# Second FFN of a macaron block: normalized rows stored by quarters and turned on VectorE instead of TensorE

## The chip, the cores and the metric

The kernel runs on one core of a Trainium2 chip. A core has TensorE for matmuls (PE in the profile; PEld is its loading of weights, which overlaps the matmuls), VectorE (DVE), ScalarE (ACT), GpSimd (POOL), and SyncE (SP), which here only issues DMAs. Each engine works through its own queue of instructions in order and waits on semaphores for the others. Matmuls write to PSUM, which here is cut into eight banks of 128 x 512 floats; everything else lives in SBUF (128 partitions) or in DRAM. The metric is the time of one execution in microseconds.

## The reference

2048 rows of 1024 channels go through three residual steps. `ffn` and `attn` normalize their input by row first.

```
x = x + 0.5 * ffn(layernorm(x))
x = x + attn(layernorm(x))
x = x + 0.5 * ffn(layernorm(x))

ffn(x):   routing = softmax(x @ gate_w.T)                 # 8 experts
          out = (x * (routing @ in_channel_scale)) @ sign(weight).T
          out = out * (routing @ out_channel_scale) + bias
attn(x):  3-tap convolution 1024 -> 768, split in q, k, v of 256
          16 heads of 64, causal softmax attention inside blocks of 128 rows
          o @ wo, then @ proj_w + proj_b                  # back to 1024 channels
```

The two FFNs use the same weights. Everything is float32; the large FFN product takes its rows in two float32r parts, a high one and a low one.

## The kernel before

The rows are handled in 16 tiles t of 128 rows (`NT` = 16), the channels in 8 chunks of 128 (`DC` = 8). The first FFN runs over the tiles, its normalized output goes through the convolution (a fast algorithm with eight products), and then come the attention and the second FFN, which the change touches.

**Attention.** It has four groups g of four tiles, and per group four turns r, each of which handles four heads (two head pairs). `turn(g, r, ...)` issues the stages of several pairs at once, staggered: `stage_qk` (q and k by seven products, accumulated in two banks "mm" and two banks "tr" and evicted by ScalarE, `put`, and VectorE, `more`), `stage_wo` of an earlier pair, `stage_transpose`, `stage_scores` (scores, masking on GpSimd, maxima on VectorE, exps on ScalarE, normalization on VectorE), `stage_values`. In turn 1 of group g, `stage_proj` finishes the previous group: for each of its four tiles two products `pp` with `proj_w`, which VectorE adds to the row tile `xr` in SBUF (L1116); the sum goes to DRAM as `x3[t]` (L1119). The row tiles are loaded by `load_residual` into the pool `rring` (4 buffers), and the DMAs of GpSimd add `proj_b`. In the same turn `signs` loads two chunks of the FFN weights into the pool `aside` (2 buffers), and ScalarE takes their signs.

**Second FFN.** `Ffn` (L188) does for each tile:

- `norm`: load the row tile from `x3` (`load_rows2`, L928), statistics on VectorE (L167, L171, L173), the power -0.5 and the shift on GpSimd (L174, L185), the normalized row `xn` on ScalarE (L186);
- `add_bias`: a DMA of GpSimd adds `hbias` to the row tile in place (L212);
- `transpose`: 8 TensorE transposes of 128 x 128 into two PSUM banks (L220), copied by ScalarE to `xnT` (L221), a tile with channels on partitions, in a pool of three buffers;
- `gate`, `route`, `turn`: the router's logits (`lgp` L228, `lg` L241), their maximum `nm` and softmax (VectorE and ScalarE), its weights `rhl` in two parts (L252, L253), turned by one TensorE transpose `rt` (L260) and copied to `rT` by VectorE (L262);
- `scale`: the input scales `is` by matmul (L272); VectorE multiplies `xnT` by them in place (L283), ScalarE rounds the product to the high part of `y` (L285), GpSimd subtracts to get the low part (L286); the output scales `po` (L295) are halved by ScalarE (L297);
- `main`: 32 matmuls `pm` of 128 x 512 (L311) in two halves of the output columns; VectorE multiplies by the output scale (L323) and adds to the row (L324); `store` writes the tile out.

`run` puts these stages in a software pipeline. In the turn of tile t:

```python
self.on(self.gate, t + 2)             # if not done yet
self.scale(t + 1, out=True)
self.main(t, 0)
self.on(self.route, t + 2)
self.on(self.transpose, t + 3)
self.on(self.norm, t + 4, t < self.kept)
self.on(self.add_bias, t + 4)
self.main(t, 1, beside={DC - 2: lambda: self.on(self.turn, t + 2)})
```

The first tiles' stages are written by hand between the stages of the last attention pairs (`ffn.transpose(0, ...)`, `ffn.gate(0)` and so on). Row tiles of the second FFN live in nine buffers: 2 of `aside`, 3 of a pool `rring2`, 4 of `rring`.

**What sets the order.** TensorE's order is written by hand (`manual_schedule`). The other engines' queues are filled by a planner that takes instructions by program order, priority and its own estimate of when each is ready; so an instruction may move ahead of others on its engine. A tile in a pool gets the buffer of the tile that many places before it, and its first writer waits for the last reader of that one.

## Time and profile before

| | |
|---|---|
| median of three runs | 940.13 us (940.07 to 940.71) |
| the profiled execution | 940.06 us, span 938.3 us |
| granted TensorE clock | 1.00 of full speed |
| 0 to 200 us, first FFN: TensorE busy | 189.6 us |
| 200 to 540 us, convolution and the start of attention: TensorE busy | 337.9 us |
| 540 to 740 us, attention: TensorE busy, of each 40 us | 39.7 to 40.0 us |
| second FFN in its steady part, one tile (pm at 900.61 to pm at 910.49) | 9.88 us |
| transposes of the second FFN on TensorE | 128, of 273 ns each, overlapping |

The span is what the profiler recorded from the first to the last instruction of one execution; about 1.8 us of the time lie around it. A line of the timeline gives the start and the duration in us, the engine, the line of the kernel, the operation, output<-input, shapes and a count, and in brackets how long the engine had idled and for whom. Consecutive instructions of one kind are merged, with the time from the first's start to the last's end. A line of groups gives a count, the busy time in us and the mean in ns of one. Matmul rows are pipelined, so their durations overlap: what one costs is read from the starts around it. L numbers are those of this kernel.

### The profile page before, as it was taken

Reading aid. Unit: us, or ns where it says so; the run is one execution under the profiler, and the core shown is the slowest. Engines: PE = TensorE matmul, PEld = TensorE weight load, DVE = VectorE, ACT = ScalarE, POOL = GpSimd, SP = SyncE. Lnnn points to the kernel's source line nnn. Section 1 sums busy time; section 2 is a strip of 40 time slices with the busy share of each in tenths; the row PEclk is TensorE's granted clock in tenths of the full one; section 3 lists DMA queues with packets and bytes.
Section 4 is the critical chain, followed back from the end, with each engine's and each line's share of the span. In section 5 each row is a group of like instructions: output and inputs, shape, how many; then the busy total and the mean of one; then the engine's idle time right before and its main releaser. Section 6 shows DMA issues by size and latency. Waiting matters only on the chain.

```text
span 938.3 us, 14525 instructions
## 1 busy us (share of the span) xinstructions
PE 920.0 (98%) x5240; PEld 659.5 (70%) x5240; DVE 662.3 (71%) x1326; ACT 462.0 (49%) x1258; POOL 235.7 (25%) x330
## 2 busy tenths in 40 slices
PE   6999999999999999999999999999999999999998
PEld 4678878886666666675876577567765756788786
DVE  5888887789978677656686557656746666666654
ACT  5676666431111111126886567666855844454441
POOL 2554453220011100101231113013201404444341
PEclk9999999999999999999999999999999999999999
DMA  9776653499567765536360245032406737655341
GB/s 343 181 199 192 178 182 136 186 274 353 181 201 195 190 188 135 117 108 222 116 135 23 75 154 133 23 140 89 88 1 209 150 114 210 172 163 152 90 114 67
DMA packets 39543, 144.86 MB, mean 154 GB/s; under 512 B 5096, under 2 KB 6120, under 8 KB 37552
## 3 DMA queue, kind: packets, MB, share of 16 engines
q1 hardware_dynamic: 28048, 97.91, 28.9%
q0 software_dynamic: 10688, 38.02, 20.9%
q10 hardware_dynamic: 736, 8.02, 2.3%
q8 instruction: 41, 0.67, 0.3%
q14 instruction: 30, 0.25, 0.1%
HBM read 89.30 MB, written 37.85 MB: 136 GB/s over the span
## 4 chain that ended last, share of the span: by engine, by line
PE 80%; DVE 7%; ACT 6%; DMA 3%; issue 3%; POOL 1%; POOLq 0%; DVEq 0%; ACTq 0%
PE cv L544 23%; PE pm_f L311 19%; PE pq L829 7%; PE pp L1108 6%; PE pv L829 5%; PE acc L1084 4%; PE sc L1012 3%; PE tr_f L220 3%; PE pt L1054 2%; DMA x<-in_x_dram 2%; ACT p L1039 2%; PE ao L1067 2%; PE lgp_f L228 2%; PE is_f L272 1%; ACT qk L972 1%
## 5 line engine op out<-in xcount | busy, mean ns | idle before, releaser
L311 PE MATMUL pm_f<-sw,y_f 128*128 128x512 f32 x1024 | 258.4, 403 | 0.6 <-ACT y_f L285 0.4
L311 PEld LDWEIGHTS pm_f<-sw,y_f 128*128 128x128 f32 x1024 | 186.8, 190 | 41.9 <-ACT y_f L285 0.8
L544 PE MATMUL cv<-v,u 128*128 128x342 f32 x576 | 166.0, 450 | 0.0
L544 PEld LDWEIGHTS cv<-v,u 128*128 128x128 f32 x576 | 109.2, 190 | 56.7
L1025 POOL TENSOR_SCALAR_AFFINE_SELECT p<-p 128x512 f32<-128x512 f32 x64 | 38.5, 635 | 249.6 <-ACT p L1021 249.6
L1039 ACT ACTIVATE p<-p,anm 128x128 f32<-128x128 f32 x256 | 99.8, 396 | 0.0
L561 ACT ACTIVATE m<-cv 128x342 f32<-128x342 f32 x42 | 19.2, 456 | 154.4 <-PE cv L544 152.3
L323 DVE TENSOR_TENSOR pm_f<-pm_f,os_f 128x512 f32<-128x512 f32 x64 | 44.6, 697 | 68.6 <-PE pm_f L311 68.5
L286 POOL TENSOR_TENSOR y_f<-xnT_f,y_f 128x512 fp32r<-128x512 f32 x63 | 80.0, 1288 | 45.3 <-ACT y_f L285 45.3
L1035 DVE TENSOR_REDUCE anm<-p 128x4 f32<-128x512 f32 x64 | 39.6, 678 | 26.9 <-POOL p L1025 26.9
L1084 PE MATMUL acc<-oT,wo_sb 128*128 128x512 f32 x128 | 58.0, 595 | 0.2 <-DVE oT L1076 0.2
L544 PE MATMUL cv<-v,g 128*128 128x342 f32 (+2 forms) x224 | 57.1, 415 | 0.8 <-DVE v L466 0.8
L1108 PE MATMUL pp<-pw_sb,o2T 128*128 128x512 f32 x128 | 56.4, 596 | 0.0
L221 ACT COPY xnT_f<-tr_f 128x512 f32<-128x512 f32 x58 | 33.6, 588 | 41.6 <-PE tr_f L220 39.9
L544 PEld LDWEIGHTS cv<-v,g 128*128 128x128 f32 x224 | 39.7, 190 | 17.6 <-DVE v L466 1.2
L1039 ACT ACTIVATION_READ_ACCUMULATOR p<-p,anm 128x1 f32 x256 | 49.9, 195 | 0.0
L1059 DVE COPY pT<-pt 128x512 f32<-128x512 f32 x32 | 22.1, 690 | 38.8 <-PE pt L1054 38.8
L972 ACT ACTIVATE qk<-pq,sbq 128x256 f32<-128x256 f32 x64 | 30.0, 469 | 39.5 <-PE pq L829 39.5
L1047 DVE TENSOR_TENSOR p<-p,asum 128x512 f32<-128x512 f32 x64 | 45.1, 704 | 1.3
L1108 PEld LDWEIGHTS pp<-pw_sb,o2T 128*128 128x128 f32 x128 | 23.7, 190 | 29.1 <-issue 26.1
L297 ACT ACTIVATE os_f<-po_f 128x512 f32<-128x512 f32 x64 | 34.8, 595 | 16.8 <-PE is_f L272 6.7
L285 ACT CAST y_f<-xnT_f 128x512 fp32r<-128x512 f32 x64 | 37.6, 626 | 11.1 <-DVE xnT_f L283 11.1
(186 smaller groups left out, 1668.0 us busy)
## 6 DMA issues: line engine op xcount, KB each, us to landing
g<-in_conv_w_dram SPq DMA_DIRECT2D x28, 512.0 KB, 5.2
u<-in_conv_w_dram POOLq DMA_DIRECT2D x24, 512.0 KB, 6.1
x<-in_x_dram SPq DMA_DIRECT2D x16, 512.0 KB, 5.5
raw<-in_weight_t_dram SPq DMA_DIRECT2D x16, 512.0 KB, 6.5
x<-hbias POOLq DMA_DIRECT2D x16, 512.0 KB, 5.3
x<-x SPq DMA_DIRECT2D x16, 512.0 KB, 4.1
xr<-x SPq DMA_DIRECT2D x16, 512.0 KB, 4.9
xr<-in_proj_b_dram POOLq DMA_DIRECT2D x16, 512.0 KB, 9.1
```

Source lines behind the costliest of these rows:

```text
L286: lows[h].tensor_tensor(yl, y, yh.bitcast(F32), ALU.subtract)
L311: ins = nc.tensor.matmul(pms[h], lhsT=y[:, n, c, :], rhs=self.sw[:, c, ts(h, NB)], start=(c == 0 and n == 0), stop=(c == DC - 1 and n == 1),)
L323: nc.vector.tensor_tensor(pms[h], pms[h], o, ALU.mult)
L544: nc.tensor.matmul(accs[w, k][:, lo:hi], lhsT=uk[:, c, :], rhs=V[k][:, c, lo:hi], start=(c == 0), stop=(c == DC - 1),)
L829: nc.tensor.matmul(leave.sums[sums], lhsT=rows[a][:, u, :], rhs=cols[b], start=n in (0, 1, 3), stop=True, skip_group_check=True,)
L972: nc.scalar.activation(h, acc, AF.Identity, bias=bias, scale=(QSCALE, 1.0)[n])
L1025: nc.gpsimd.affine_select(out=p, in_=p, pattern=[[0, BPG], [-1, P]], compare_op=ALU.is_ge, fill=NEG_INF, base=0, channel_multiplier=1,)
L1035: nc.vector.tensor_reduce(nmax, p, AX.X, ALU.max, negate=True)
L1039: exps[g, r] = nc.scalar.activation(p[:, b, :], p[:, b, :], AF.Exp, bias=nmax[:, b : b + 1], accum_out=asum[:, b : b + 1],)
L1047: nc.vector.tensor_tensor(p, p, asum.unsqueeze(2).broadcast_to([P, BPG, P]), ALU.mult)
L1084: nc.tensor.matmul(accs[g][m], lhsT=wo_sb[:, hp, ts(m, P)], rhs=oT, start=(hp == 0), stop=(hp == NHP - 1),)
L1108: nc.tensor.matmul(pp, lhsT=o2T[:, m, ts(b, P)], rhs=pw_sb[:, m, ts(h, NB)], start=(m == 0), stop=(m == WC - 1),)
```

## The change

The rows are no longer normalized in the second FFN but in attention, right after `stage_proj` has finished them: VectorE takes the statistics of `xr` there (`row_statistics`), and ScalarE writes the normalized row to a tile `xp`, in an order that puts quarters of 32 channels of each chunk together. Four DMAs per tile store `xp` to DRAM (`quarters[t]`) so that quarter q of all channels lies on partitions 32q to 32q + 31. The second FFN loads such a tile (`xl`, three buffers) in one DMA, and two VectorE instructions per tile turn it in blocks of 32 x 32, which gives the same `xnT` as the eight TensorE transposes and two copies did. The row tiles `xf` have seven buffers instead of nine, since `xp` and `xl` take room; `aside` holds `xp` in the first three groups, and two buffers of a new pool in the last one. In the compiled kernel VectorE's two transposes of a tile often stand well ahead of their place in the program, as the planner sets them.

```diff
--- before.py
+++ after.py
@@ -368,6 +368,42 @@
 
 
 
+    class Second(Ffn):
+        def load(self, t):
+            xl = self.xns[t] = self.xnp.tile([P, 4, DC, QC], F32, name=f"xl_{self.name}_{t}", tag="xn")
+            nc.sync.dma_start(out=xl, in_=quarters[t].rearrange("p (t j a) -> p t j a", t=4, j=DC))
+        def transpose(self, t):
+            xl = self.xns.pop(t)
+            xnT = self.work.tile([P, DC, P], F32, name=f"xnT_{self.name}_{t}", tag="xnT", bufs=3)
+            blocks = xnT.rearrange("p j (t b) -> p t j b", t=4)
+            for k in range(2):
+                nc.vector.transpose(blocks[:, ts(k, 2)], xl[:, ts(k, 2)])
+            self.xnTs[t] = xnT
+        def run(self, first):
+            for t in range(first, self.end):
+                self.on(self.gate, t + 2)
+                if t + 1 < self.end:
+                    self.scale(t + 1, out=True)
+                self.main(t, 0)
+                self.on(self.route, t + 2)
+                self.on(self.transpose, t + 3)
+                self.on(self.beside, t + NT - 2)
+                self.on(self.ahead, t + 4)
+                self.main(t, 1, beside={DC - 2: lambda: self.on(self.turn, t + 2)})
+                self.on(self.after, t - 1)
     NK = 8
     SCALES = (1.0, -2.0 / 9, -2.0 / 9, 1.0 / 90, 1.0 / 90, 1.0 / 180, 1.0 / 180, 1.0)
     PAIRS = ((1, 2), (3, 4), (5, 6))
@@ -922,13 +958,13 @@
     f2 = ctx.enter_context(ExitStack())
     rring = pool(b3, "rring", BPG)
     aside = pool(b3, "aside", 2)
-    rows, x3 = {}, {}
+    rows, x3, quarters = {}, {}, {}
     later = []
 
     def load_rows2(t):
         if t in rows:
             return
-        pl = aside if t % 9 < 2 else later[0] if t % 9 < 5 else rring
+        pl = aside if t % 7 < 2 else later[0] if t % 7 < 3 else rring
         rows[t] = pl.tile([P, D], F32, name=f"xf_{t}", tag="x")
         nc.sync.dma_start(out=rows[t], in_=x3[t])
 
@@ -1100,6 +1136,45 @@
                 pin(nc.sync.dma_start(out=rows[t], in_=x2[t]))
                 pin(nc.gpsimd.dma_start(out=rows[t], in_=proj_b.broadcast_to([P, D]), accum_op=ALU.add))
 
+        finish = {}
+        def row_statistics(t):
+            src = rows[t]
+            stats = small.tile([P, NH2, 6], F32, name=f"st_f2_{t}", tag="stats")
+            for h in range(NH2):
+                nc.vector.bn_stats(out=stats[:, h, :], in_=src[:, ts(h, NB)])
+            mv = small.tile([P, 2], F32, name=f"mv_f2_{t}", tag="mv")
+            nc.vector.bn_aggr(out=mv, in_=stats)
+            rstd = small.tile([P, 1], F32, name=f"rs_f2_{t}", tag="rstd")
+            nc.vector.tensor_scalar(rstd, mv[:, 1:2], EPS, None, ALU.add)
+            nc.gpsimd.tensor_tensor(rstd, rstd, nhalf, ALU.pow)
+            shift = small.tile([P, 1], F32, name=f"sh_f2_{t}", tag="shift")
+            nc.gpsimd.tensor_scalar(shift, mv[:, 0:1], rstd, -1.0, ALU.mult, ALU.mult)
+            def normalized():
+                pl = later[1] if t + BPG >= NT else aside
+                xp = pl.tile([P, D], F32, name=f"xp_{t}", tag="x")
+                nc.scalar.activation(
+                    xp.rearrange("p (q j a) -> p j q a", q=4, j=DC),
+                    src.rearrange("p (j q a) -> p j q a", q=4, j=DC),
+                    AF.Identity,
+                    bias=shift,
+                    scale=rstd,
+                )
+                quarters[t] = spill.tile([P, D], F32, name=f"xq_{t}")
+                to = quarters[t].rearrange("(q b) c -> b q c", q=4)
+                for k in range(4):
+                    nc.sync.dma_start(
+                        out=to[:, :, ts(k, D // 4)],
+                        in_=xp[ts(k, QC), :].rearrange("b (q c) -> b q c", q=4),
+                    )
+            finish[t] = normalized
         def stage_proj(g, b, kinds=("mm", "tr")):
             o2T = accs[g]
             for h in range(NH2):
@@ -1115,6 +1190,7 @@
                 xt = rows[g * BPG + b][:, ts(h, NB)]
                 stored[g] = nc.vector.tensor_tensor(xt, pp, xt, ALU.add)
             t = g * BPG + b
+            row_statistics(t)
             x3[t] = spill.tile([P, D], F32, name=f"x3_{t}")
             nc.sync.dma_start(out=x3[t], in_=rows.pop(t))
 
@@ -1139,6 +1215,9 @@
             if r == 1 and g + 1 < NG:
                 tokens_of(g + 1)
             stage_qk(g, r)
+            if r > 1 and g > 0:
+                with tc.high_priority(offset=300):
+                    finish.pop((g - 1) * BPG + r)()
             if r == 0 and g > 0:
                 load_residual(g - 1)
             if r == 1:
@@ -1162,52 +1241,51 @@
             if r == 1 and g > 0:
                 for b in range(BPG):
                     stage_proj(g - 1, b)
+                    if b > 1:
+                        finish.pop((g - 1) * BPG + b - 2)()
 
         with tc.manual_schedule(engines={mybir.EngineType.PE}):
             for i in range(LAST - 1):
                 turn(*divmod(i, NP), True)
-                if i == LAST - 3:
-                    for t in range(2):
-                        load_rows2(t)
                 if i == LAST - 2:
                     load_residual(NG - 1)
             g, r = pairs[-1]
-            begun = {}
-            xn_of = {}
+            stage_qk(g, r)
+            with tc.high_priority(offset=300):
+                finish.pop(g * BPG - 1)()
             for t in range(2):
-                with tc.issue_after(stored[g - 1].ins):
-                    begun[t] = sums_of(
-                        lambda t=t: xn_of[t], rows[t], f"f2_{t}", on_vector=t, later=True
-                    )
-            stage_qk(g, r)
+                load_rows2(t)
 
             b2.close()
             pool(f2, "edge2", 1, side="right").tile([P, 120], F32, name="right_edge2")
             work = pool(f2, "work2", 2, side="right")
-            xn2 = pool(f2, "xn2", 3, side="right")
-            later.append(pool(f2, "rring2", 3, side="right"))
-            ffn = Ffn("f2", sw2, work, xn2, 0, NT, lambda t: rows[t], load_rows2, store, lambda t: None, lambda t: None, NT, leave)
+            xlp = pool(f2, "xl2", 3, side="right")
+            later.append(pool(f2, "rring2", 1, side="right"))
+            later.append(pool(f2, "xp2", 2, side="right"))
+            def begin_tile(t):
+                ffn.load(t)
+                load_rows2(t)
+                ffn.add_bias(t)
+            def finish_row(t):
+                finish.pop(t, lambda: None)()
+            ffn = Second("f2", sw2, work, xlp, 0, NT, lambda t: rows[t], begin_tile, store, None, finish_row, NT, leave)
+            for t in range(3):
+                ffn.load(t)
             two(stage_wo, LAST - 3)
             two(stage_transpose, LAST - 2, "sm", "tr")
-            for t in range(2):
-                ffn.xns[t] = xn_of[t] = xn2.tile([P, D], F32, name=f"xn_f2_{t}", tag="xn")
-                begun[t]()
-
-            def begin_tile(t):
-                ffn.norm(t, t > 0)
-                ffn.add_bias(t)
-
-            on_vector = (nc.vector.tensor_copy,) * 2
+            ffn.transpose(0)
             stage_scores(g, r)
             with tc.high_priority(offset=400):
                 two(stage_values, LAST - 2)
             for t in range(2):
                 ffn.add_bias(t)
-            ffn.transpose(0, on_vector)
             two(stage_wo, LAST - 2)
             ffn.gate(0)
             stage_transpose(g, NHP - 2, "sm")
-            ffn.transpose(1, on_vector)
+            ffn.transpose(1)
             stage_values(g, NHP - 2)
             stage_transpose(g, NHP - 1, "mm")
             stage_wo(g, NHP - 2)
@@ -1216,16 +1294,19 @@
             ffn.gate(1, "tr")
             stage_wo(g, NHP - 1)
             with tc.issue_after(ended[g].ins):
-                begin_tile(2)
+                load_rows2(2)
+                ffn.add_bias(2)
             one = ("mm", "mm")
             stage_proj(g, 0, one)
             ffn.turn(0)
             ffn.transpose(2)
             stage_proj(g, 1, one)
             ffn.scale(0, out=True)
+            finish_row(NT - 4)
             ffn.route(1)
             stage_proj(g, 2, one)
             stage_proj(g, 3, one)
+            finish_row(NT - 3)
             ffn.turn(1)
             begin_tile(3)
     ffn.run(0)
```

## The prediction

> **What bounds the kernel now.** I read the page's busy times first, then the timeline of the second FFN, then that of the attention stage in front of it, and last the waits.

> ```profile
> PE 920.0 (98%) x5240; PEld 659.5 (70%) x5240; DVE 662.3 (71%) x1326; ACT 462.0 (49%) x1258; POOL 235.7 (25%) x330
> PEclk9999999999999999999999999999999999999999
> PE 80%; DVE 7%; ACT 6%; DMA 3%; issue 3%; POOL 1%; POOLq 0%; DVEq 0%; ACTq 0%
> ```

> TensorE is busy for 98% of the span at full granted clock: work taken from it shortens the run, unless a wait takes its place. So the question is what TensorE's order will wait for. The timeline of the second FFN shows two tiles that differ in just what the change touches. At 904.52 stand the last eight transposes; the tile that starts at 910.49 (t = 13) has none, and no normalization beside it:

> ```profile
> 904.38 0.28 PE L241 MATMUL lg_f<-fold,lgs_f 128*128 128x8 f32 x2
> 904.52 1.07 PE L220 MATMUL tr_f<-ident,xn_f 128*128 128x128 f32 x8
> 905.34 3.01 PE L311 MATMUL pm_f<-sw,y_f 128*128 128x512 f32 x12
> ...
> 910.49 3.93 PE L311 MATMUL pm_f<-sw,y_f 128*128 128x512 f32 x16
> 910.77 1.28 DVE L283 TENSOR_TENSOR xnT_f<-xnT_f,is_f 128x512 f32<-128x512 f32 x2
> 912.33 2.53 POOL L286 TENSOR_TENSOR y_f<-xnT_f,y_f 128x512 fp32r<-128x512 f32 x2 [7.16 <-ACT y_f L285]
> 914.26 0.28 PE L241 MATMUL lg_f<-fold,lgs_f 128*128 128x8 f32 x2
> 914.40 2.99 PE L311 MATMUL pm_f<-sw,y_f 128*128 128x512 f32 x12
> 914.46 0.70 DVE L323 TENSOR_TENSOR pm_f<-pm_f,os_f 128x512 f32<-128x512 f32 x1 [2.41 <-PE pm_f L311]
> ...
> 916.28 0.29 DVE L253 SCALAR_TENSOR_TENSOR rhl_f<-ro_f,rsum_f,rhl_f 128x64 fp32r<-128x64 f32 x1
> 917.23 0.27 PE L260 MATMUL rt_f<-ident,rhl_f 128*128 128x128 f32 x1
> ```

> From the lg matmul to the next pm matmul it is 0.96 us with transposes and 0.14 without: eight cost 0.82 us. The routing weights rhl are ready at 916.57 and TensorE takes them (rt) at 917.23: 0.66 us in hand, no more. GpSimd ends its subtractions, the last readers of xnT, at 914.86.

> **The change, part by part.** The sum is made against the profiled run's 940.06 us (span 938.3 and 1.8 around it), the median of the runs shown being 940.13.

> *Transposes off TensorE.* 16 tiles x 0.82 = -13.1 us, 3 of the tiles before the loop, 13 in it. ScalarE also loses 1.24 + 2 x 0.59 us a tile in this stage, where it idles anyway: nothing.

> *Transposes on VectorE, in the loop.* Two 128x512 instructions a tile. No row shows one. Bounds: 0.54 us (TENSOR_SCALAR 128x512, SBUF to SBUF, mean 542) and 1.22 (SCALAR_TENSOR_TENSOR 128x1024, mean 1216, as if each element took two cycles). I take 0.64, the pace of BATCH_NORM_STATS2, which also reads 512 elements of SBUF and takes 1.28 for two. They replace 1.28 + 0.21 + 0.15 us of statistics, so VectorE's load hardly changes; their place does. In the compiled order of VectorE the two transposes of tile t+4 stand directly behind the two multiplications of tile t+1 (L283), ahead of the pm multiplication, in t = 1, 3 and 5 to 11. xnT has three buffers, so tile t+4 writes where tile t+1 lies, and must wait until GpSimd's second subtraction has read it. Counted from the tile's first pm matmul: GpSimd ends at 914.86 - 910.49 = 4.37; handing over takes 0.06, the transposes 1.28, to 5.71; from the start of the pm multiplication to the end of rhl it took 2.11 (914.46 to 916.57), to 7.82, and 0.05 to TensorE: 7.87. TensorE is at rt at 917.23 - 910.49 = 6.74. It waits 1.13 us, which is 0.31 more than the transposes cost. The four pm matmuls behind rt, and with them the next tile, move along. Nine tiles: +10.2. In t = 4 the planner puts 14 instead of 12 pm matmuls ahead of rt, which leaves 0.65. In t = 0 is_1 comes after four pm matmuls, so GpSimd ends later: 1.8. In t = 2 the pair stands around the pm multiplication of half 1, costs no rt wait, but delays by 0.64 the multiplications that t = 3 then waits for: +0.64. Together +13.3 (5.7 us more or less for each 0.25 us of one transpose).

> [...]

> *Start of the FFN.* VectorE does six transposes ahead of oT_6 where it did four copies (mean 669): +1.2 us; and the maxima anm_3_1 now stand behind the reciprocal of p_6_0's sums, which holds the exps back by 1.0. By the rows from 747.72 on I get the ao_7 matmuls 2.0 us later than before, though 1.64 us of TensorE transposes are gone ahead of them: 3.6 lost. Then the first transpose of tile 3 stands ahead of the second pp_2 addition and waits for GpSimd's subtractions of tile 0 (2.49 long); pp_3's second matmuls need that PSUM bank: 2.2. With the statistics of rows 14 and 15 between, rT_1 comes 0.8 later. Together +6.6. Bounds: 0 (other work covers it all) and 10, if the first quarters loaded land 3 us late: 3.5 MB of loads at 98 MB per 271 us (28.9% of the span) take 10 us and share the engines with the proj_b additions.

> *Attention, groups 1 to 3.* VectorE gets 1.28 + 0.21 + 0.15 us of statistics a row beside the pp additions, ScalarE one normalization a row (1.24), SP four stores of 128 KB a row and later a load (0.32 us each to issue).

> ```profile
> 620.78 0.68 DVE L1047 TENSOR_TENSOR p<-p,asum 128x512 f32<-128x512 f32 x1
> ...
> 628.14 0.69 DVE L1116 TENSOR_TENSOR xr<-pp,xr 128x512 f32<-128x512 f32 x1 [1.02 <-PE pp L1108]
> 629.86 0.69 DVE L1116 TENSOR_TENSOR xr<-pp,xr 128x512 f32<-128x512 f32 x1 [1.02 <-PE pp L1108]
> ...
> 630.29 0.47 ACT L972 ACTIVATE qk<-pq,sbq 128x256 f32<-128x256 f32 x1 [6.92 <-PE pq L829]
> 630.96 0.59 PE L829 MATMUL pq<-x,wk_sb 128*128 128x256 f32 x2
> ```

> VectorE is busy without a gap until 623.7 and then has 1.02 us free per addition of 1.72; the 1.64 a row fits two such gaps, but row 0's share adds to the busy stretch. Followed through, the last pp addition ends at 631.8 instead of 630.55, and the pq matmul at 630.96 needs its bank: 0.9 us a group, 2.7 in all. ScalarE's first two normalizations fall into its 6.92 us of idling; the third stands among the qk evictions, where it idles 1.69; the fourth delays a copy of scores by 1.24, but the probabilities it holds back are multiplied behind the column sums (655.65) in two groups and have 0.4 us and TensorE's earlier pt to spare in the third: nothing. If this cover fails, each costs 1.24 us, 14.9 for twelve. Bounds 0 and 14.9; I take 2.7, since the backlog follows from rows of this stage. GpSimd's 0.56 + 0.26 a row and the selects queued behind them: it idles 26.64 us there. What waits on SP behind the stores are residual loads and tokens needed ten microseconds and more later; the third normalization needs its `aside` buffer back from the stores, 2.6 us to land by the output's row.

> *Row buffers.* Nine become seven: xf of t+7 waits for the store of t (2.6), its load (4.5), then GpSimd's bias DMA (0.90), which stands ahead of y. From 0.4 into the next tile that leaves some 3 us before GpSimd is needed. Costed at nothing; later than that, it costs one for one on about six tiles. The quarters are loaded more than a tile ahead, 4.5 us in tiles of 10.

> Sum: 940.1 - 13.1 + 13.3 + 6.6 + 2.7 = 949.6. I say 949.5.

> **The rivals.** *The waits stay off the path (faster).* If the transposes let the pm multiplication through, because GpSimd ends earlier or the instruction is very short, the 13.1 us stay: with the attention's 2.7 and a quarter of the start (1.6), 931.3. For it: VectorE has 2.41 us free ahead of the pm multiplication. Against it: GpSimd's end at 4.37 lies 0.4 behind that multiplication's start (3.97). The point that decides: waits below (13.1 - 9.3) / 11.5 = 0.33 us a tile.

> *The transpose takes 1.22 us.* VectorE's chain to rt grows by 1.16: 11.5 x 1.16 = 13.3 more in the loop and 2.3 at the start: 965. Nothing but the missing row speaks for it.

> *Attention pays more.* If half of the normalizations fall on the path, or the small stores return `aside` late, 7.5 us more, with 1 for late quarters: 958. For it: ScalarE is busy 5.00 of 5.00 us around 615 and 645. Against it: its idle times above.

> *It cancels.* With 0.54 us a transpose and the start free, 940 - 13.1 + 10 + 2.7 = 940: no change.

> **How the numbers follow.** My case 0.53 (its own range 944 to 956), waits off the path 0.22, dear transpose 0.08, dear attention 0.12, cancelled 0.05. About 0.2%, 1.9 us, is what a measurement of this kernel can tell from no change. Faster: 0.22 and 0.02 of the cancelled: 0.24; same 0.05; slower 0.71. The range 932 to 962 leaves out half of the fast rival and most of the dear transpose, some 0.18.

> **What would show it.** Right: no tr_f in the second FFN; transposes of about 0.6 to 0.7 us on VectorE that idle for GpSimd first; TensorE's rt waiting some 1.1 us for rhl in nine tiles; tiles of about 10.2 us against 9.88; pp_3 and oT_6 late. Wrong: tiles near 9.1 us with rt not waiting; a transpose far from 0.64; TensorE gaps in the attention stage over 3 us a group; a bias DMA of GpSimd, or a load of quarters, ahead of the wait.

## The result

The changed kernel takes 954.18 us (median of 4 runs, 953.63 to 955.24) against 940.1 us before (939.93 to 940.71, 4 runs): a ratio of 1.015 with a 95% interval of 1.0132 to 1.0168. It is slower, as forecast, and 4.7 us slower than the 949.5 forecast, inside the range. The profiled execution took 954.39 us, with a span of 952.6. Below, "shift" is the start of an instruction on TensorE in this trace, minus the start of the same instruction in the trace of before.

From the page of the changed kernel, the lines that answer to those shown of before: busy times, the granted TensorE clock in 40 slices, and the chain that ended last by engine.

```profile
PE 913.5 (96%) x5112; PEld 649.3 (68%) x5112; DVE 671.9 (71%) x1353; ACT 451.8 (47%) x1231; POOL 236.2 (25%) x331
PEclk9999999999999999999999999999999999989999
PE 69%; DVE 9%; DMA 7%; issue 6%; POOL 5%; ACT 5%; SPq 0%; POOLq 0%; DVEq 0%; ACTq 0%
```

TensorE has 128 instructions less, as it should, but its share of the chain falls from 80% to 69%. More of the chain now runs over VectorE (9% for 7), DMA (7 for 3), GpSimd (5 for 1) and "issue" (6 for 3). One slice of the clock line is new too: the 8.

A steady tile of the second FFN (the turn t = 9, whose rt belongs to tile 11) in the timeline of the changed kernel:

```profile
885.35 1.28 DVE L283 TENSOR_TENSOR xnT_f<-xnT_f,is_f 128x512 f32<-128x512 f32 x2
886.98 2.53 POOL L286 TENSOR_TENSOR y_f<-xnT_f,y_f 128x512 fp32r<-128x512 f32 x2 [2.93 <-ACT y_f L285]
888.83 0.28 PE L241 MATMUL lg_f<-fold,lgs_f 128*128 128x8 f32 x2
888.96 2.99 PE L311 MATMUL pm_f<-sw,y_f 128*128 128x512 f32 x12
889.54 1.31 DVE L387 STREAM_TRANSPOSE xnT_f<-xl_f 128x512 f32<-128x512 f32 x2 [2.91 <-POOL y_f L286]
890.77 0.67 DVE L323 TENSOR_TENSOR pm_f<-pm_f,os_f 128x512 f32<-128x512 f32 x1
...
892.56 0.28 DVE L253 SCALAR_TENSOR_TENSOR rhl_f<-ro_f,rsum_f,rhl_f 128x64 fp32r<-128x64 f32 x1
...
892.99 0.30 PE L260 MATMUL rt_f<-ident,rhl_f 128*128 128x128 f32 x1 [1.04 <-DVE rhl_f L253]
```

VectorE idles 2.91 us for GpSimd's subtractions, with the pm multiplication queued behind the transposes; when those are through, rhl comes 1.04 us too late for TensorE. From lg to the next pm matmul it is now 0.13 us instead of 0.96. A tile takes 10.24 us (rt at 882.75 and 892.99) against 9.88 before.

The largest single loss lies elsewhere, in t = 4. First GpSimd's part of the timeline, then TensorE's, then windows of two microseconds (length, TensorE's busy time and instructions, granted clock, DMA share, GB/s):

```profile
828.05 0.86 POOL L212 DMA_DIRECT2D xf<-hbias  x1 [3.48 <-issue]
834.10 0.86 POOL L212 DMA_DIRECT2D xf<-hbias  x1 [5.19 <-DMA xf<-x]
834.66 2.83 POOL L286 TENSOR_TENSOR y_f<-xnT_f,y_f 128x512 fp32r<-128x512 f32 x2
```

```profile
840.84 0.45 PE L260 MATMUL rt_f<-ident,rhl_f 128*128 128x128 f32 x1 [3.92 <-DVE rhl_f L253]
```

```profile
838.00:840.00 2.00, 0.00 (x0) 0.93 1.05 258
840.00:842.00 2.00, 1.16 (x3) 0.50 0.74 244
842.00:844.00 2.00, 2.00 (x27) 0.50 0.52 190
844.00:846.00 2.00, 2.00 (x7) 0.50 0.98 193
846.00:848.00 2.00, 2.00 (x9) 0.86 0.99 324
```

A bias DMA of a later tile stands ahead of the subtractions of tile 5 in GpSimd's queue. It waits until 834.10 for the load of its row, the subtractions begin at 834.66 (with the bias DMA behind them, as the run `bias_behind_y` has it, they begin at 831.90), and everything of the steady chain follows from there: TensorE stands for 3.92 us. Its clock is granted at half from 839.7 to 846.6, most of that after it has started again.

The start of the second FFN in the changed kernel, VectorE first, then TensorE, and last the same ao matmuls in the kernel before, where they waited for nothing:

```profile
757.80 0.71 DVE L387 STREAM_TRANSPOSE xnT_f<-xl_f 128x512 f32<-128x512 f32 x1 [1.50 <-DMA xl_f<-xq]
758.43 0.65 DVE L1083 TENSOR_TENSOR p<-p,asum 128x512 f32<-128x512 f32 x1
...
761.62 1.31 DVE L387 STREAM_TRANSPOSE xnT_f<-xl_f 128x512 f32<-128x512 f32 x2 [0.68 <-DMA xl_f<-xq]
```

```profile
761.00 1.80 PE L1103 MATMUL ao<-pT,vh 128*64 128x128 f32 x14 [2.92 <-DVE pT L1095]
...
785.58 1.98 PE L1183 MATMUL pp<-pw_sb,o2T 128*128 128x512 f32 x4 [1.95 <-DVE xr L1191]
```

```profile
756.43 1.09 PE L1067 MATMUL ao<-pT,vh 128*64 128x128 f32 x16
```

The quarters of tiles 1 and 2 are late, and the probabilities of the last attention pair are queued behind their transposes. The second stop, of pp, is the one the prediction worked out.

Where the time went, by shifts. "Start" is what is left of the shift at rt of tile 1 (+7.42) after the attention's 1.22 and with the 2.46 us of transposes of three tiles added back.

| part | predicted, us | in this trace, us |
|---|---|---|
| transposes off TensorE, 16 x 0.82 | -13.1 | -13.1 |
| attention (shift at 740) | +2.7 | +1.2 |
| start of the FFN | +6.6 | +8.7 |
| loop, t = 0 to 3 | +4.7 | +3.8 |
| loop, t = 4 and 5 | +1.8 | +6.7 |
| loop, t = 6 to 11 | +6.8 | +7.1 |
| loop, t = 12 | 0 | 0 |
| sum | +9.5 | +14.4 |

(In the loop rows each tile's 0.82 is added back to what its shift grew by. From rt to rt the shift grew by 3.71 in t = 4 and 1.31 in t = 5. In t = 4 two more pm matmuls, 0.51 us, stand ahead of rt than before, so the tiles themselves lost 4.22 and 0.80, where the prediction's terms give -0.17 and +0.31. Of the 6.7 us of the two tiles the wait is 3.92; the 5.7 us at half clock behind it are, as an estimate, 2.6, since pm matmuls start 0.43 us apart there, at 844.72 to 846.42, and 0.23 apart from 846.72 on at full clock; that leaves 0.2.)

### The profile page after: what moved, and what is told of

Same layout as the page of the kernel before. It is cut to its first block, busy times and chain, and to the rows that moved or that the text cites. A ratio compares the mean times of both kernels' runs of the same rounds, so it can differ in the third digit from the quotient of the medians.

```text
span 952.6 us, 14379 instructions
## 1 busy us (share of the span) xinstructions
PE 913.5 (96%) x5112; PEld 649.3 (68%) x5112; DVE 671.9 (71%) x1353; ACT 451.8 (47%) x1231; POOL 236.2 (25%) x331
## 4 chain that ended last, share of the span: by engine, by line
PE 69%; DVE 9%; DMA 7%; issue 6%; POOL 5%; ACT 5%; SPq 0%; POOLq 0%; DVEq 0%; ACTq 0%
PE cv L580 23%; PE pm_f L311 13%; PE pq L865 7%; PE pv L865 5%; PE pp L1183 5%; PE acc L1120 4%; PE sc L1048 2%; POOL y_f L286 2%; DMA x<-in_x_dram 2%; PE ao L1103 2%; PE pt L1090 2%; DMA xl_f<-xq 2%; DMA xf<-x 1%; PE lgp_f L228 1%; PE is_f L272 1%
## 5 line engine op out<-in xcount | busy, mean ns | idle before, releaser
L311 PE MATMUL pm_f<-sw,y_f 128*128 128x512 f32 x1024 | 261.1, 405 | 0.6 <-ACT y_f L285 0.4
L311 PEld LDWEIGHTS pm_f<-sw,y_f 128*128 128x128 f32 x1024 | 188.3, 191 | 41.4 <-ACT y_f L285 0.8
L286 POOL TENSOR_TENSOR y_f<-xnT_f,y_f 128x512 fp32r<-128x512 f32 x63 | 80.2, 1294 | 79.4 <-ACT y_f L285 79.3
L323 DVE TENSOR_TENSOR pm_f<-pm_f,os_f 128x512 f32<-128x512 f32 x64 | 44.3, 692 | 42.7 <-PE pm_f L311 42.4
L387 DVE STREAM_TRANSPOSE xnT_f<-xl_f 128x512 f32<-128x512 f32 x32 | 21.4, 694 | 39.9 <-POOL y_f L286 37.7
L285 ACT CAST y_f<-xnT_f 128x512 fp32r<-128x512 f32 x64 | 37.6, 624 | 12.0 <-DVE xnT_f L283 11.9
L568 DVE SCALAR_TENSOR_TENSOR u<-g,u 128x1024 f32<-128x1024 f32 x18 | 22.0, 1224 | 29.1 <-DMA u<-in_conv_w_dram 11.7
```

The lines of the kernel that those rows point to most:

```text
L285: copy(yh, y)
L286: lows[h].tensor_tensor(yl, y, yh.bitcast(F32), ALU.subtract)
L311: ins = nc.tensor.matmul(pms[h], lhsT=y[:, n, c, :], rhs=self.sw[:, c, ts(h, NB)], start=(c == 0 and n == 0), stop=(c == DC - 1 and n == 1),)
L323: nc.vector.tensor_tensor(pms[h], pms[h], o, ALU.mult)
```

## The experiments

Medians, with the ratio to the kernel before on the same chip (940.3, 941.0 or 940.6 us there):

| run | us (lowest to highest) | ratio to before, 95% interval |
|---|---|---|
| t_behind_rhl | 937.72 (935.63 to 942.51) | 0.9982 (0.9964 to 0.9999) |
| bias_behind_y | 951.86 (950.51 to 953.11) | 1.0128 (1.0111 to 1.0145) |
| start_order | 951.89 (950.7 to 954.73) | 1.0128 (1.0109 to 1.0147) |
| three_orders | 931.6 (930.89 to 932.1) | 0.9907 (0.9893 to 0.9922) |
| fourth_xnT | 941.22 (939.06 to 944.49) | 1.0006 (0.9996 to 1.0016) |
| fourth_xnT_bias | 935.74 (933.82 to 937.78) | 0.9948 (0.9929 to 0.9966) |
| attention_alone | 942.05 (941.81 to 942.7) | 1.0013 (1.0004 to 1.0023) |
| made_gaps | 950.22 (one) | - |
| orders_less_traffic | 930.39 (one) | - |
| tile0_later | 931.37 (931.01 to 931.64) | 0.9902 (0.9885 to 0.9918) |

### The transposes behind rhl

```diff
+            self.last = nc.vector.scalar_tensor_tensor(          # in Ffn.route: the second part of rhl
                 rhl[:, :, 1, :], copies, ...
...
-                self.on(self.transpose, t + 3)                   # in Second.run
+                with tc.issue_after(self.last.ins):
+                    self.on(self.transpose, t + 3)
```

`issue_after` makes the instructions inside it follow the named one in their engine's queue.

> In the loop the two transposes of tile t+3 are queued directly behind rhl of tile t+2, where the program writes them, instead of behind the is-multiplications; nothing else is moved. Theory (the waits of TensorE at rt come from this order: VectorE waits for GpSimd's second subtraction with the pm multiplication queued behind it): the rt waits of the loop go, tiles fall from 10.24 to about 9.1 us, and so does the wait of pp_3 for the transposes of tile 3 (2.2 us). Against the changed kernel: 17.1 us of loop waits and 2.2 at its start less, about 935 us. Rival (VectorE has no room for the transposes anywhere, and the wait turns up again at rT or at lgp): less than a third of this is won, 948 us or more.

Measured: 937.72 us, 16.5 less than the changed kernel and at or just below the kernel before (the interval ends at 0.9999). Of the loop's ten rt waits one is left (1.57 us, t = 4), and pp_3's wait falls from 1.95 to 0.63 us. VectorE's timeline of a steady tile:

```profile
873.92 0.70 DVE L323 TENSOR_TENSOR pm_f<-pm_f,os_f 128x512 f32<-128x512 f32 x1 [2.40 <-PE pm_f L311]
...
875.75 0.29 DVE L253 SCALAR_TENSOR_TENSOR rhl_f<-ro_f,rsum_f,rhl_f 128x64 fp32r<-128x64 f32 x1
875.95 1.30 DVE L387 STREAM_TRANSPOSE xnT_f<-xl_f 128x512 f32<-128x512 f32 x2
```

In the profiled execution, the fastest of the ten (935.63 us), the shift falls by 0.85 us a tile, so tiles take 9.03 us. Why others take up to 942.51 no trace shows. The theory holds: the same transposes at the same price, one place further back in the queue, cost TensorE nothing. VectorE had the room.

### A fourth buffer instead of another place

The order of the changed kernel is kept, but the tile that is turned no longer lies where GpSimd reads.

```diff
-            xnT = self.work.tile([P, DC, P], F32, ..., tag="xnT", bufs=3)     # in Second.transpose
+            xnT = self.work.tile([P, DC, P], F32, ..., tag="xnT", bufs=4)
...
+                with tc.issue_after(self.scaled.ins):            # the last is-multiplication
+                    self.on(self.transpose, t + 4)
                 self.main(t, 0)
                 self.on(self.route, t + 2)
-                self.on(self.transpose, t + 3)
...
-            later.append(pool(f2, "xp2", 2, side="right"))
+            later.append(pool(f2, "xp2", 1, side="right"))
```

Quarters are loaded at t + 5 instead of t + 4.

> In the changed kernel's order (transposes of tile t+4 directly behind the is-multiplications of tile t+1) xnT gets a fourth buffer, so that this tile does not lie where GpSimd still reads; the place for it comes from one of the two xp2 buffers, and quarters are loaded one tile earlier. Theory (what costs time is the wait for GpSimd in front of the pm multiplication, not the place or the work of the transposes): VectorE has 2.41 us free ahead of that multiplication and the pair takes 1.30, so no rt waits from it, tiles of 9.1 us, and 935 to 939 us. Rival (the place itself delays rhl by the pair's 1.3 us): 0.6 us of rt wait a tile stays, 943 us or more.

Measured: 941.22 us, between the two. Two rt waits (2.02 and 1.84 us) and one pm wait (1.30) are left in the loop, and none of them is the wait of the changed kernel; tiles without them take 9.03 us. One of them, in GpSimd's, VectorE's and TensorE's timeline:

```profile
820.01 0.87 POOL L212 DMA_DIRECT2D xf<-hbias  x1 [7.83 <-DMA xf<-x]
820.61 2.80 POOL L286 TENSOR_TENSOR y_f<-xnT_f,y_f 128x512 fp32r<-128x512 f32 x2
```

```profile
820.53 2.95 DVE L252 TENSOR_SCALAR rhl_f<-ro_f,rsum_f 128x64 fp32r<-128x64 f32 x1
823.51 0.28 DVE L253 SCALAR_TENSOR_TENSOR rhl_f<-ro_f,rsum_f,rhl_f 128x64 fp32r<-128x64 f32 x1
```

```profile
823.94 0.30 PE L260 MATMUL rt_f<-ident,rhl_f 128*128 128x128 f32 x1 [2.02 <-DVE rhl_f L253]
```

The rhl multiplication, 0.256 us in the median of this stage, took 2.95 us and ended 0.07 us after GpSimd's subtractions did. At 860.42 the same took 2.77 us and ended at 863.19, GpSimd's subtractions at 863.13. So a bias DMA that holds GpSimd up does its harm in a second way, without any transposes waiting. That was put to the test with the bias DMAs moved in this kernel too (the edit of the next section):

> The kernel with the fourth xnT buffer, and GpSimd's bias DMAs queued behind the subtractions as in the run that moved them alone. Theory (what was left in the loop there came from GpSimd: a bias DMA waited for a row's load, the subtractions began late, and ran while VectorE wanted to multiply rhl, whose 0.25 us instruction then took 2.95 and 2.77): the two rt waits (2.02, 1.84) and the wait of pm for y (1.30) go, 5.2 us, 936 us, and no rhl multiplication of the loop over 1 us. Rival (the long rhl multiplications have another cause, such as the transposes ahead of them): they stay, 940 us or more.

Measured: 935.74 us. The wait of pm and one of the two long multiplications are gone; the other is left at 2.17 us, with 1.24 us of rt wait, since one bias DMA that waits for its row's load (until 819.47, with GpSimd idle for 7.04 us) still stands ahead of tile 4's subtractions. The theory's sum holds (936), its "none over 1 us" does not.

### GpSimd's bias DMAs behind its subtractions

```diff
-                lows[h].tensor_tensor(yl, y, yh.bitcast(F32), ALU.subtract)           # in Ffn.scale
+                self.low = lows[h].tensor_tensor(yl, y, yh.bitcast(F32), ALU.subtract)
...
-                self.on(self.ahead, t + 4)                                            # in Second.run
+                with tc.issue_after(self.low.ins):
+                    self.on(self.ahead, t + 4)
```

> GpSimd's bias DMA of tile t+4 is queued behind the two subtractions of tile t+1; the transposes stay where the changed kernel has them. Theory (the 3.9 us stop of TensorE in t = 4 comes from a bias DMA that stands ahead of the subtractions of tile 5 and waits for its row's load, and the clock of 0.50 behind it comes from that stop): t = 4 costs 1.1 us of wait like its neighbours instead of 4.5 with 1.9 behind it, so about 949 us, and no slice of the second FFN below full clock. Rival (DMA traffic itself holds up tile 5 and lowers the clock): the stop moves to another wait, 953 us or more.

The same place of GpSimd's timeline in the profile of this run, and TensorE's windows:

```profile
831.90 2.53 POOL L286 TENSOR_TENSOR y_f<-xnT_f,y_f 128x512 fp32r<-128x512 f32 x2 [6.89 <-ACT y_f L285]
834.38 0.86 POOL L212 DMA_DIRECT2D xf<-hbias  x1
```

```profile
836.00:838.00 2.00, 0.97 (x6) 1.00 0.97 197
838.00:840.00 2.00, 2.00 (x29) 1.00 1.05 240
840.00:842.00 2.00, 2.00 (x16) 1.00 1.02 367
```

The rt wait of t = 4 is 1.03 us, like its neighbours', with the clock at 1.00, at DMA shares around 1 again. From rt of tile 5 to rt of tile 7 it takes 20.47 us instead of 24.78: 4.3 us are won there, not the 5.3 that the expectation added up. The median is only 2.3 us lower, between the two expected values. The place and the mechanism are shown; why the median gains less than the trace is not. The four runs' mean granted clocks (0.998, 0.998, 0.996, 0.993) fall as their times rise (950.5, 951.1, 952.6, 953.1), but that settles nothing: the three fastest of the 13 executions of the kernel before beside them (939.81 to 939.93) have 0.993 too. Only one of the four has a trace, and in that one the clock fell at the start of the FFN, to 0.50 in 762 to 764.

### The order at the start

```diff
-            ffn.transpose(1)
+            with tc.issue_after(turned[g, NHP - 2].ins):         # VectorE's copy pT_6_1
+                ffn.transpose(1)
...
-            ffn.transpose(2)
+            with tc.issue_after(evicted[g, NHP - 1].ins):        # the eviction oT_7
+                ffn.transpose(2)
```

> At the start of the second FFN the transposes of tile 1 are queued behind the pT_6_1 copy and those of tile 2 behind the eviction oT_7; the loop is left alone. Theory (the start lost 4.1 us because transposes that wait for late quarters stand ahead of the p multiplications and pT copies): ao_6 to pt_7 gets its 4.1 us back, and the 0.8 us of lower clock behind it: about 949 us. Rival (the start is limited by something else, the six transposes' own 3.9 us on VectorE or the loads of pT's users): less than 1.5 us, 952.5 or more.

Measured: 951.89 us, neither. The stop of 2.92 us at ao is gone, but in the profiled execution another of 2.83 us stands in front of lgp, because tile 0's quarters land later there (its transposes begin at 755.59, after 1.21 us of waiting for them) and the p multiplications are queued behind those transposes; the clock falls after this stop as it did after the other. The order was one part; the quarters' lateness is the other. Where it comes from was tried on the kernel with all three edits, with the last group's four proj_b additions left out (rows 12 to 15 lack proj_b):

> The three edits together, with the four proj_b additions of the last group left out (2 MB read, 2 MB of row buffers rewritten, so rows 12 to 15 lack proj_b); the order of the transposes stays, but for those of tile 0, which come two multiplications later. Theory (the quarters are late because the loads around them share full DMA engines): the median landing of the six quarters loaded between 735 and 790 falls from 13.5 us by several us. Rival (a load of quarters is slow by itself, by its short rows or its place in the queue): above 12 us still.

DMA issues between 735 and 790 us (queue, count, KB each, median us from issue to landing), with the additions and then without:

```profile
xl_f<-xq SPq DMA_DIRECT2D x6, 512.0 KB, 13.7
```

```profile
xl_f<-xq SPq DMA_DIRECT2D x6, 512.0 KB, 8.0
```

The quarters land 5.7 us sooner when 2 MB of additions are not there: they are late because they share engines that are full (the DMA share is 1.04 to 1.08 in every window from 750 to 764 of the changed kernel). The time hardly changes, 930.39 against 931.6 us: with the transposes queued where they block nothing, lateness costs little. (This is one execution, 0.5 us below the lowest of the four with the additions.)

### All three

The three edits above together: transposes behind rhl, bias DMAs behind the subtractions, the order at the start.

> The three edits together. Theory (three independent queueing mistakes and nothing else beside the 13.1 us of transposes and 1.3 us of attention): 954.2 - 17.1 - 2.2 - 4.9 = 930 us, below the kernel before by about 1%; granted clock 1.0 throughout; rt waits for nothing. Rival (the edits overlap or the DMA limit shows once the queues are clear): above 935 us.

Measured: 931.6 us, ratio 0.9907 (0.9893 to 0.9922): faster than the kernel before by 0.9%. Its page (granted clock, chain by engine) and its steady tile:

```profile
PEclk9999999999999999999999999999999999999999
PE 79%; DVE 6%; issue 5%; ACT 4%; DMA 3%; POOL 3%; POOLq 0%; DVEq 0%; ACTq 0%
```

```profile
885.62 2.53 POOL L286 TENSOR_TENSOR y_f<-xnT_f,y_f 128x512 fp32r<-128x512 f32 x2 [5.68 <-ACT y_f L285]
887.68 0.70 DVE L323 TENSOR_TENSOR pm_f<-pm_f,os_f 128x512 f32<-128x512 f32 x1 [2.41 <-PE pm_f L311]
...
889.50 0.28 DVE L253 SCALAR_TENSOR_TENSOR rhl_f<-ro_f,rsum_f,rhl_f 128x64 fp32r<-128x64 f32 x1
889.71 1.30 DVE L387 STREAM_TRANSPOSE xnT_f<-xl_f 128x512 f32<-128x512 f32 x2
890.45 0.27 PE L260 MATMUL rt_f<-ident,rhl_f 128*128 128x128 f32 x1
890.93 0.25 DVE L262 CAST rT_f<-rt_f 128x128 fp32r<-128x128 f32 x1
```

VectorE waits for TensorE again (2.41 us), not the other way round; the transposes lie between rhl and the copy of rt, and TensorE's rt waits for nothing. The shift against before is +2.76 at rt of tile 1, falls by 1.1 and 1.0 in the first two tiles and by 0.85 in each further one, to -8.72. The medians' gains of the three edits alone are 16.5, 2.3 and 2.3 us, 21.1 together; all at once they bring 22.6.

One more step on this kernel: tile 0's transposes are queued later too, and its lgp matmuls after acc_6.

> The kernel of the three edits, and the transposes of tile 0 queued behind the pT_6_1 copy as well, tile 1's behind pT_7_1, with the lgp matmuls of tile 0 behind the ao_6 and acc_6 matmuls on TensorE. Theory (the last transposes on the path are tile 0's 1.3 us ahead of the p multiplications): lgp's wait of 1.58 goes and 1.3 us are won, 930.3 us. Rival (routing of tile 0 is then late for rt, or the p multiplications wait for the exps anyway): 931.6 us or more.

Measured: 931.37 us, no difference (0.37 us in the profiles). lgp's wait is gone, but ao_6 then waits 1.59 us for ScalarE's copy of pT. The time is the rival's; what stands there is ScalarE's copy.

### The attention part alone

The kernel before, with `row_statistics` called as in the changed kernel for the row tiles 0 to 11 and `normalized` for 0 to 9; nothing reads the quarters.

```diff
+            if g < NG - 1:
+                row_statistics(t)
             x3[t] = spill.tile([P, D], F32, name=f"x3_{t}")
...
                     stage_proj(g - 1, b)
+                    if b > 1:
+                        finish.pop((g - 1) * BPG + b - 2)()
```

> The kernel before, with the attention part of the change alone: statistics, normalization and the four stores of quarters for rows 0 to 9, which nothing reads; its second FFN is untouched. Theory by the changed kernel's landmarks (1.33 us by 740): about 941 us. Theory of the prediction (0.9 us a group for a PSUM bank of pq): about 942.3 us, with a gap of TensorE ahead of a pq matmul. Rival (the attention part also costs the start of the FFN, by traffic): 944 or more.

Measured: 942.05 us, ratio 1.0013 (1.0004 to 1.0023), so 0.4 to 2.2 us. TensorE's waits between 560 and 745 us in this run (engine, line, what it waited for: us in total, times, longest):

```profile
PE pt L1054 <- DVE asum L1046: 0.7, 2, 0.4
PE pq L829 <- DVE qk L976: 0.5, 1, 0.5
PE pt L1054 <- DVE p L1047: 0.4, 2, 0.2
PE pq L829 <- ACT vh L998: 0.3, 2, 0.2
```

Small waits of the probabilities' transposes and of one pq; before, the same stretch has 0.5 us (pt for p) and 0.3 (pq for vh). The wait of 0.5 us of pq for VectorE is of the kind that the prediction built on, once and not in each group; in the changed kernel's trace no pq waits for VectorE in this stretch. The shift at 740 is 2.4 us in this run's trace, of which some 0.7 stand ahead of the attention's added work (0.1 or less in the changed kernel), so this part costs 1.7 us here and 1.2 there.

### Stops made on purpose

The kernel before, with VectorE's copy pT of one head pair repeated in three places; the extra copies write the same values.

```diff
-                    nc.vector.tensor_copy(pT, pt)
+                    for _ in range({(1, 2): 4, (2, 2): 6, (3, 2): 9}.get((g, hp), 1)):
+                        nc.vector.tensor_copy(pT, pt)
```

> The kernel before, with one copy on VectorE repeated 3, 5 and 8 times more in three places of the attention stage (groups 1, 2 and 3), so that TensorE stands idle there for some 1.5, 3 and 5 us; no traffic is added. Theory (TensorE's granted clock falls by itself after a stop of about 2.5 to 3 us, and the falls of the changed kernel are consequences of its two stops): no fall after the first, falls to 0.5 for some 4 us after the third and perhaps the second. Rival (the falls come with full DMA traffic): 1.0 throughout.

The first place made no stop, the second 1.72 us, the third 5.36 us. The third ends at 740.16. Windows of one microsecond around it (length, TensorE's busy time and instructions, granted clock, DMA share, GB/s):

```profile
736.00:737.00 1.00, 0.00 (x0) 1.00 0.00 0
737.00:738.00 1.00, 0.00 (x0) 0.59 0.29 41
738.00:739.00 1.00, 0.00 (x0) 0.50 1.00 188
...
743.00:744.00 1.00, 1.00 (x7) 0.50 1.00 188
744.00:745.00 1.00, 1.00 (x5) 1.00 1.11 221
```

The clock falls some 2.4 us into the stop, out of a stretch of next to no traffic, and comes back 3.8 us after TensorE started again. After the 1.72 us it stays at 1.00. So a stop alone is enough, and the falls of the changed kernel, each behind a stop of 2.9 us or more, need no other cause. And full traffic alone is not enough: with the DMA share at 1.00 to 1.09 from 752 to 770, the run with the transposes behind rhl keeps 1.00 throughout.

## Why the prediction was right, and where it was not

- *Transposes off TensorE, -13.1.* Right: 0.82 to 0.85 us a tile, so 0.10 us each.
- *The price of one transpose, 0.64.* Right. The group of the changed kernel (busy us, mean ns of one, idle time before):

```profile
L387 DVE STREAM_TRANSPOSE xnT_f<-xl_f 128x512 f32<-128x512 f32 x32 | 21.4, 694 | 39.9 <-POOL y_f L286 37.7
```

A single one is recorded with 0.69, a pair with 1.30.
- *The wait of rt in the steady tiles, 1.13.* Right in place, cause and size: in seven of the nine tiles 0.98 to 1.04 us of idling as the trace records it, 10.24 us a tile where about 10.2 were forecast. (t = 3 has more by forecast, and in t = 5 the clock was low.) That it is the queue's order around GpSimd's subtraction, and not VectorE's load, is shown from two sides: another place (t_behind_rhl) and another buffer (fourth_xnT) each take it away.
- *t = 0 and t = 3.* Both waits are there, 1.61 and 1.34 us; over t = 0 to 3 the loop lost 0.9 less than forecast.
- *Row buffers "costed at nothing", and t = 4 at 0.65.* This is the step that failed, and with t = 5 it cost 4.9 us more than forecast. It counted one bias DMA per tile, ahead of its y, and 3 us to spare, with loads that land after 4.5 us. In the compiled order a bias DMA of a later tile stands ahead of tile 5's subtractions, and with full DMA engines the row loads landed after 6.1 us (median, 800 to 840). The prediction named "a bias DMA of GpSimd ahead of the wait" among what would show it wrong, but its sum had looked for it at the steady tiles alone; it is the first tiles after the start, where loads pile up, that pay. bias_behind_y shows it. The sum also had no term for the clock, whose half speed behind this stop is, by the estimate above, 2.6 of the 6.7 us.
- *Start of the FFN, +6.6.* Mechanism partly right, size too small: +8.7. The wait of pp_3 came as worked out (2.2 forecast; from rt_0 to rt_1 it took 13.64 us instead of 12.30 with 0.82 of transposes gone, so 2.2 longer). The bound "the first quarters loaded land 3 us late" should have been in the sum: between 735 and 790 us the quarters took 13.5 us to land, and p and pT were queued behind them. Behind the stop of 2.92 us the clock stood at half from 761.2 to 764.6, for which the sum had no term either.
- *Attention, +2.7.* Too much: 1.2 by the changed kernel's shifts, 0.4 to 2.2 by the run of that part alone. In the changed kernel the bank of pq that the step was built on held nothing up.
- *The rivals.* The waits did not stay off the path; the version in which they do runs at 931.6, near the rival's 931.3, so it was three changes of order away. That the two figures agree so well is partly luck: by its shifts that version lost 1.9 up to 740 (0.6 of it ahead of the attention's added work) and 3.4 at the start and gained 0.8 more in the loop, where the rival had 2.7, 1.6 and nothing.

Too little by 4.9 for the bias DMA, 2.1 for the start and 0.3 for t = 6 to 11, too much by 1.5 for attention and 0.9 for the first tiles: 4.9 us, where the forecast's sum (949.6) and the profiled execution (954.4) are 4.8 apart. So the terms that fell short miss 7.3 us, and it is luck that 2.4 of that were covered by terms that were too large.

## What to carry to other kernels

When work is moved to an engine with free time, look at what is queued behind it: here two instructions of 0.65 us, set ahead by the planner, had VectorE idle for 2.91 us a tile for GpSimd's read of their buffer, and TensorE's rt, which needs what stood behind them, waited 1.04 us; queued behind rhl they cost TensorE nothing (three_orders). Check the same for DMAs that wait for other DMAs in an engine's queue, at the busiest place and not in the steady tile. If the price of the moved work fits and only waits are new, reorder before giving up: here the same instructions in other places are worth 22.6 us.
